# Graph block with experts on one core: edge lists kept in DRAM, deeper look-ahead in the middle stage, and the last node tile taken first

## The chip, the cores and the metric

The program runs on one core of a Trainium2 chip. The core has five engines with their own instruction lists: TensorE (PE, with its weight loads as PEld), VectorE (DVE), ScalarE (ACT), GpSimd (POOL) and SyncE (SP), which issues most of the transfers. The metric is the device time of one execution in microseconds (us), and the number compared is the median over runs. All times below are in us unless ns is written.

## The reference, cut to what matters

There are 6250 nodes with 256 features, 200000 edges sorted by destination, and 8 experts.

```python
xn = _layernorm(x)
x = x + gnn(edge_index, xn) + mix(xn)
x = x + ffn(_layernorm(x))

def gnn(A, X, W, b):                   # self-loops are added to A
    deg  = segment_sum(ones, dst)
    norm = rsqrt(deg)[src] * rsqrt(deg)[dst]
    return relu(segment_sum((X @ W)[src] * norm[:, None], dst) + b)

def mix(x):                            # linear attention, one sequence of all nodes
    q, k, v = split(x @ Wqkv.T);  q = elu(q) + 1;  k = elu(k) + 1
    t  = q @ sum(k v^T) / (q . sum(k) + 1e-6)       # per head, 8 heads of 32
    x1 = layer_norm(t + x)
    return layer_norm(gelu(x1 @ W1.T + b1) @ W2.T + b2 + x1)

def ffn(h):                            # one expert per token, capacity 977
    idx  = argmax(softmax(h @ gate_w + gate_b))
    pos  = running count of the tokens with that expert, in token order
    kept = pos < 977                   # the others get nothing
    return prob * expert[idx](h) * kept             # 256 -> 1024, relu -> 256
```

The running count ties the routing to the order of the tokens: which tokens fall beyond an expert's capacity depends on their place in the sequence, so tiles have to be routed in ascending order.

## The kernel before

The nodes lie in 49 tiles of 128 (tile 48 has 106 nodes). `twos` pairs them into 25 groups: group g holds tiles 2g and 2g+1, and the last group holds tile 48 alone. The program has three stages.

*Stage one* runs to about 295 us. It reads x, takes the layer norm's statistics, makes q, k and v (q goes to DRAM as `q_dram`), finds where each node's edges begin, and writes the normed, degree-scaled node rows to DRAM as `g_dram` (512 columns: the value in a high and a low part). It also makes the edge lists. For odd tiles these are `idx` (which row of `g_dram` to fetch) and `rel` (its place in the tile), and for even tiles `hiT` and `loT` (which source tile and which row in it, 110 columns for five tiles and each half). In the kernel before these four lists lie on chip for the whole of the main part. ScalarE copies each finished piece from PSUM into its list. Stage one ends with a flag, read from the device, and a branch (`tc.If`): when an edge list doesn't fit the fast form, a slow general path computes the sums instead and the lists are filled with values that match nothing. With these inputs the slow path isn't taken.

*Stage two* (about 300 to 1646 us) sums the neighbours' rows into every tile and finishes the nodes. Three generators share the engines, and the schedule is manual: within an engine, instructions run in the order in which the generators' steps are called.

- `gather()`, for the 24 odd tiles: 34 slots (EB) per tile, 816 in all. In slot j POOL issues an indirect DMA that fetches 128 rows into `gt` (L891) and VectorE makes a one-hot matrix `oh` from `rel` (L895). LAG slots later PE adds `oh` x `gt` into the PSUM tile `ps` (L906). A tile's sum starts with two matmuls of the tile's own rows (L903, L904). After slot 34, `put_sum` copies the left half out with ScalarE (L825) and adds the right half with VectorE (L827). The pool `ga` has GB buffers for `gt` and `oh`, the PSUM pool `gaps` has two for `ps`.
- `dense()`, for the 25 even tiles: a dense matrix of edge counts, tile by all 6250 source nodes, is built from one-hot pairs and then multiplied with all rows, which lie on chip in `xs3`. A unit (one tile) is 11 steps. In each step VectorE makes four pairs `lo`, `hi` (L838, L840), PE multiplies those of the step before into two PSUM banks `bp` (four matmuls, L874), ScalarE copies the banks into the matrix `A` (L875), and in the next unit PE does some 15 of the 147 matmuls `ps_d` (L858) of the matrix that is complete.
- `rounds()`: one round takes a group whose sums are there (c) through the GNN's matrix (L1067), layer norm and gate, the next group (b) through the second layer norm, and the one after it (a) through attention (L1099) and the MLP, each round being some 20 steps with `yield` between them. After every two groups `routing` turns the gate's values into slots of the experts' buffer and scatters the tokens to `xbuf` with one indirect DMA per tile (L984). Group 24, tile 48 alone, has a round and a routing of its own at the very end.

The loop that interleaves them calls one gather step per slot, and as many dense steps and round steps as keep the pace:

```python
        while any(alive.values()):
            step("g", G)
            while alive["d"] and done_d * (NGT + LAG) < n_dense * (j + 1):
                ...
            while alive["s"] and done_s < SIDE * (j + 1):
                ...
            j += 1
```

*Stage three* (from 1689 us) reads the experts' counts (L1207), loads each expert's tokens and weights, and computes two layers per expert (L1257, L1267), with a scatter to the output at the end (L1285).

Of the kernel before, what the change touches and what calls it, by code (L numbers as in the profile page):

```python
# [46 lines left out]
GB = 9  # L47
LAG = 7
SIDE = 0.74
# [13 lines left out]
def graph_block_kernel(  # L63
# [32 lines left out]
    deg_dram = dram.tile([AGR, 1], F32, name="deg_dram")  # L96
    q_dram = dram.tile([len(twos), P, 2, 2 * P], F32, name="q_dram")
# [3 lines left out]
    lists = main.enter_context(tc.tile_pool(name="lists", bufs=1))  # L101
    idx = lists.tile([P, NGC * P], I32, name="idx")
    rel = lists.tile([P, NGC * P], F32, name="rel")
    hiT = lists.tile([P, NDC, 2, 5 * NG], F32, name="hiT")
    loT = lists.tile([P, NDC, 2, 5 * NG], F32, name="loT")
# [356 lines left out]
    def edge_lists():  # L462
# [55 lines left out]
        for c in range(NGC):  # L518
            if c % 4 == 0:
                et = [rps.tile([P, 512], F32, name="et_ps", tag="et_ps", bufs=2) for _ in range(2)]  # L520
            gd, gs = got.pop(c)
            gf, gf2 = gd.bitcast(F32), gs.bitcast(F32)
            V.tensor_scalar(gf, gd, nfirst[:, c:c + 1], None, op0=OP.subtract)
            V.tensor_copy(gf2, gs)
            yield
            for e, w in zip(et, (gf, gf2)):
                nc.tensor.transpose(e[:, c % 4 * P:(c % 4 + 1) * P], w, ident)
            ask(c + 2)
            yield
            if c % 4 == 3 or c == NGC - 1:  # L530
                for o, e in zip((rel, idx), et):
                    nc.scalar.copy(o[:, (c - c % 4) * P:(c + 1) * P], e[:, :(c % 4 + 1) * P])
                yield
        for c in range(NDC):
# [18 lines left out]
            for v, o in ((kf, hiT), (lf, loT)):  # L553
                et_ps = rps.tile([P, 512], F32, name="et_ps", tag="et_ps", bufs=2)
                for h in range(2):
                    nc.tensor.transpose(et_ps[:, h * W:(h + 1) * W], v[:W, h * P:(h + 1) * P], ident[:W, :W])
                nc.scalar.copy(o[:, c].rearrange("p h g -> p (h g)"), et_ps[:, :2 * W])
# [150 lines left out]
    with tc.If(flag == 1):  # L708
        with tc.tile_pool(name="gp", bufs=1, side="right") as gp:
# [96 lines left out]
            V.memset(rel, -1.0)  # L806
            V.memset(hiT, 400.0)
# [3 lines left out]
    with tc.tile_pool(name="ga", bufs=GB, side="right") as ga, \  # L811
            tc.tile_pool(name="de", bufs=2, side="right") as de, \
            tc.tile_pool(name="gaps", bufs=2, space=PSUM) as gps, \
            tc.tile_pool(name="deps", bufs=1, space=PSUM) as dps, \
            tc.tile_pool(name="bups", bufs=2, space=PSUM) as bps, \
# [13 lines left out]

        def onehots(u, p):  # L830

            c, b = divmod(u, 5)
            o = []
            for g in (2 * p, 2 * p + 1):
                for h in range(2):
                    col = b * NG + g
                    lo = de.tile([P, P], BF16, name="lo", tag="lo", bufs=8)
                    V.tensor_scalar(lo, rowb, loT[:, c, h, col:col + 1], None, op0=OP.is_equal)  # L838
                    hi = de.tile([P, NB * GN], BF16, name="hi", tag="hi", bufs=8)
                    V.tensor_scalar(hi, hib, hiT[:, c, h, col:col + 1], None, op0=OP.is_equal)  # L840
                    o.append((lo, hi))
            return o

        def dense():

            mats, made = {}, None
            acc_ps = None
            half = NG // 2
            for u in range(ND + 1):
                for p in range(half):  # L850
                    if u >= 1 and p >= 1:

                        A = mats[u - 1]
                        if p == 1:
                            acc_ps = dps.tile([P, D], F32, name="ps_d", tag="ps_d")
                        for hi in range((p - 1) * NB // (half - 1), p * NB // (half - 1)):
                            for h in range(3):
                                nc.tensor.matmul(acc_ps, A[:, hi, :], xs3[:, hi, h * D:(h + 1) * D],  # L858
                                                 start=(hi == 0 and h == 0), stop=(hi == NB - 1 and h == 2))
                    coming = None  # L860
                    if u < ND:
                        if p == 0:
                            mats[u] = de.tile([P, NB, P], BF16, name="A", tag="A")
                        coming = (u, p, onehots(u, p))
                    if made is not None:
                        uu, pp, oh = made
                        for i in range(2):
                            g = 2 * pp + i
                            w = GN if g < NG - 2 else 4
                            at = GN * g if g < NG - 1 else P - 4  # L870
                            bp = bps.tile([P, 512], F32, name="bp", tag="bp")
                            for h in range(2):
                                lo, hi = oh[2 * i + h]
                                nc.tensor.matmul(bp[:, :NB * GN], lo, hi, start=(h == 0), stop=(h == 1))  # L874
                            nc.scalar.copy(mats[uu][:, :, at:at + w],  # L875
                                           bp[:, :NB * GN].rearrange("p (s k) -> p s k", k=GN)[:, :, :w])
                        if pp == half - 1:

                            V.tensor_tensor(mats[uu][:, 2 * uu, :], mats[uu][:, 2 * uu, :], identb, op=OP.add)
                    made = coming  # L880
                    if u >= 1 and p == half - 1:
                        put_sum(2 * (u - 1), acc_ps)
                    yield

        def gather():
            tiles = {}
            ps = None
            for j in range(NGT + LAG):
                if j < NGT:
                    gt = ga.tile([P, 2 * D], FR, name="gt", tag="gt")  # L890
                    nc.gpsimd.indirect_dma_start(  # L891
                        out=gt, out_offset=None, in_=g_dram,
                        in_offset=bass.IndirectOffsetOnAxis(ap=idx[:, j:j + 1], axis=0))
                    oh = ga.tile([P, P], FR, name="oh", tag="oh")
                    V.tensor_scalar(oh, rowb, rel[:, j:j + 1], None, op0=OP.is_equal)  # L895
                    tiles[j] = (gt, oh)
                i = j - LAG
                if i >= 0:
                    k, e = divmod(i, EB)
                    t = 2 * k + 1  # L900
                    if e == 0:
                        ps = gps.tile([P, 2 * D], F32, name="ps", tag="ps")
                        nc.tensor.matmul(ps, identb, xs3[:, t, :2 * D], start=True, stop=False)  # L903
                        nc.tensor.matmul(ps[:, D:], identb, xs3[:, t, 2 * D:], start=False, stop=False)  # L904
                    gt, oh = tiles.pop(i)
                    nc.tensor.matmul(ps, oh, gt, start=False, stop=(e == EB - 1))  # L906
                    if e == EB - 1:
                        put_sum(t, ps)
                yield
# [4 lines left out]
        def routing(batch, lgt, slots):  # L914

            tiles = [(gi, i) for gi in batch for i in range(twos[gi][1])]
            m = len(tiles)
            t0 = twos[batch[0]][0]
# [5 lines left out]
            def a3(name):  # L924
                return small([P, 4, N_EXP], name)[:, :m, :]

            def a2(name):
                return small([P, 4], name)[:, :m]
# [24 lines left out]
            fore = small([P, 5, N_EXP], "fore")  # L953
# [20 lines left out]
            for gi in batch:  # L974
# [5 lines left out]
            put = small([P, 4], "put", dtype=I32)  # L980
# [10 lines left out]
        def rounds():  # L991


            NGR = len(twos)
            xts, qs, ss, slots = {}, {}, {}, {}
            lgt = None

            def load(gi):
                if gi < NGR:
# [19 lines left out]
            for k in range(-2, NGR):  # L1019
                a = k + 2 if k + 2 < NGR else None  # L1020
                b = k + 1 if 0 <= k + 1 < NGR else None
                c = k if k >= 0 else None
# [3 lines left out]
                if a is not None:  # L1026
                    load(a + 1)
# [48 lines left out]
                if c is not None:  # L1076
                    slot = slots[c] = mx.tile([P, 2, ROW], F32, name="slot", tag="slot", bufs=3)
# [65 lines left out]
                if c is not None:  # L1143
# [5 lines left out]
                    if lgt is None:  # L1149
                        lgt, batch = small([P, 4, N_EXP], "lgt"), []  # L1150
                        if cr < P:
                            V.memset(lgt, 0.0)
                    at = 2 * len(batch)
                    batch.append(c)
# [5 lines left out]
                if c is not None:  # L1160
                    V.tensor_tensor(lgt[:cr, at:at + cn, :], lp[:cr, :cn * N_EXP].rearrange("p (t e) -> p t e", e=N_EXP),
# [12 lines left out]
                if c is not None and (len(batch) == 2 or c == NGR - 1):  # L1174
# [4 lines left out]
        n_dense = (ND + 1) * (NG // 2)  # L1179
# [11 lines left out]
        while any(alive.values()):  # L1191
            step("g", G)
            while alive["d"] and done_d * (NGT + LAG) < n_dense * (j + 1):
# [147 lines left out]
```

## Time and profile before

| | |
|---|---|
| runs, us | 2054.58, 2057.87, 2075.5; median 2057.87 |
| profiled execution, us | 2051.43, of which the span of the profile is 2049.6 |
| granted TensorE clock, mean | 0.905 |
| PE / PEld busy | 1648.4 us (80%) / 1203.4 us (59%) |
| DVE / ACT / POOL busy | 1275.3 us (62%) / 700.4 us (34%) / 924.3 us (45%) |
| moved by DMA | 337.83 MB, 165 GB/s over the span |
| costliest groups | gathers on POOL L891 794.8 us in 816; dense matmuls L858 489.4 us in 3675; one-hots `hi` L840 351.0 us in 1100; gather matmuls L906 335.1 us in 816 |

Busy shares are means over the whole span, and the three stages differ, so a share says little of what a single stage waits for. In the views of the profile a group is written as line, engine and operation, with `out<-in` by the program's names; "idle before, releaser" is the time in which the engine stood still ahead of such an instruction, with what ended it. "issue" there is time in which the engine waited for nothing that the profile shows. PEclk is the granted clock of TensorE in tenths of full speed.

### The profile page before, as it was taken

How to read it: one execution, taken by the hardware profiler on the slowest of the kernel's cores; microseconds unless marked ns; L12 is line 12 of the kernel's file. 1: busy time of each engine (PE TensorE's matmuls, PEld its weight loads, DVE VectorE, ACT ScalarE, POOL GpSimd, SP SyncE). 2: the span in 40 equal slices, each digit the busy share in tenths (PEclk: the TensorE clock that was granted, in tenths of full speed). 3: DMA queues.
4: the chain of work that ended last, by engine and by line, in shares of the span. 5: the costliest groups of instructions: out<-in, count | busy, mean ns of one | idle time of the engine just before them, and what ended most of it. 6: DMA issues, size and time to landing. Idle time of an engine off the chain costs nothing. (4 is left out here: it accounts for less than half of the span.)

```text
span 2049.6 us, 28653 instructions
## 1 busy us (share of the span) xinstructions
PE 1648.4 (80%) x9171; PEld 1203.4 (59%) x9171; DVE 1275.3 (62%) x5337; ACT 700.4 (34%) x1627; POOL 924.3 (45%) x957
## 2 busy tenths in 40 slices
PE   5787866887888888887878787887878737999996
PEld 2454544666666666665656565665656525586774
DVE  5767657677767778686757677776867431232332
ACT  2657952233333333232323232332323112233332
POOL 1022006666666666656656666665665610011111
PEclk9888997999998989898989899898999958999998
DMA  7346767777776677767767676667676615414220
GB/s 214 100 133 196 253 182 194 181 183 196 184 187 173 182 182 189 194 161 193 187 180 180 183 181 169 171 185 183 171 179 170 172 35 188 174 49 146 99 96 19
DMA packets 211319, 337.83 MB, mean 165 GB/s; under 512 B 30047, under 2 KB 79002, under 8 KB 211018
## 3 DMA queue, kind: packets, MB, share of 16 engines
q0 software_dynamic: 125424, 232.93, 44.3%
q1 hardware_dynamic: 85434, 101.74, 15.5%
q8 instruction: 81, 1.33, 0.3%
q10 hardware_dynamic: 288, 1.08, 0.1%
q14 instruction: 92, 0.75, 0.1%
HBM read 278.29 MB, written 60.06 MB: 165 GB/s over the span
## 5 line engine op out<-in xcount | busy, mean ns | idle before, releaser
L891 POOL DMA_INDIRECT gt<-g_dram,idx x816 | 794.8, 974 | 576.1 <-issue 168.7
L858 PE MATMUL ps_d<-xs,A 128*128 128x256 bf16 x3675 | 489.4, 287 | 41.3 <-issue 37.5
L875 ACT CAST A<-bp 128x294 bf16<-128x294 f32 (+1 forms) x550 | 200.6, 401 | 832.8 <-PE bp L874 231.0
L858 PEld LDWEIGHTS <-A 128*128 128x128 bf16 x3675 | 355.5, 103 | 171.5 <-issue 112.9
L906 PE MATMUL ps<-gt,oh 128*128 128x512 f32 x816 | 335.1, 484 | 42.6 <-DMA gt<-g_dram,idx 32.3
L840 DVE TENSOR_SCALAR hi<-hib,hiT 128x294 bf16<-128x294 bf16 x1100 | 351.0, 323 | 1.1 <-issue 1.1
L874 PE MATMUL bp<-hi,lo 128*128 128x294 bf16 x1100 | 216.0, 305 | 120.2 <-ACT A L875 39.6
L838 DVE TENSOR_SCALAR lo<-rowb,loT 128x128 bf16<-128x128 bf16 x1100 | 269.9, 245 | 3.2 <-PE ps_d L858 1.2
L895 DVE TENSOR_SCALAR oh<-rowb,rel 128x128 fp32r<-128x128 bf16 x816 | 207.2, 288 | 76.2 <-remote 30.4
L874 PEld LDWEIGHTS <-lo 128*128 128x128 bf16 x1100 | 109.6, 102 | 180.9 <-issue 57.3
L906 PEld LDWEIGHTS ps<-gt,oh 128*128 128x128 f32 x816 | 153.3, 206 | 76.5 <-DMA gt<-g_dram,idx 37.4
L1285 POOL DMA_INDIRECT out<-rep,who x43 | 42.4, 986 | 314.7 <-DVE rep L1283 226.8
L1257 PE MATMUL hpf<-xet,w1e 128*128 128x512 f32 (+2 forms) x544 | 154.1, 441 | 8.7 <-ACTq L1297 3.5
L1267 PE MATMUL ypf<-w2e,hm 128*128 128x256 f32 (+1 forms) x688 | 151.3, 379 | 0.0
L1267 PEld LDWEIGHTS ypf<-w2e,hm 128*128 128x128 f32 (+1 forms) x688 | 128.9, 188 | 21.9 <-issue 3.1
L1257 PEld LDWEIGHTS hpf<-xet,w1e 128*128 128x128 f32 x544 | 86.5, 193 | 70.0 <-issue 62.9
L1269 DVE TENSOR_TENSOR y<-ypf,fb_s 128x256 f32<-128x256 f32 (+1 forms) x43 | 18.2, 423 | 138.8 <-PE ypf L1267 138.8
L662 PE MATMUL mm<-wqkv_s,xnt 128*128 128x512 f32 (+1 forms) x196 | 101.5, 644 | 0.0
L1259 ACT ACTIVATE hm<-hpf,fb_s 128x512 f32<-128x512 f32 (+2 forms) x136 | 70.9, 525 | 84.6 <-PE hpf L1257 81.2
L1051 DVE TENSOR_SCALAR z<-mm 128x8 f32<-128x8 f32 (+1 forms) x49 | 7.9, 162 | 138.6 <-remote 82.6
L984 POOL DMA_INDIRECT xbuf<-slot,put x49 | 51.8, 1058 | 74.5 <-issue 45.4
L1101 ACT ACTIVATE s<-s,nb,rs 128x256 f32<-128x256 f32 (+1 forms) x98 | 53.6, 599 | 47.3 <-DVE rs_sr L194 29.8
(289 smaller groups left out, 2034.1 us busy)
## 6 DMA issues: line engine op xcount, KB each, us to landing
gt<-g_dram,idx POOLq DMA_INDIRECT x816
g_dram<-two SPq DMA_DIRECT2D x24, 512.0 KB
xt<-in_x SPq DMA_DIRECT2D x42, 256.0 KB
xbuf<-zeros SPq DMA_DIRECT2D x26, 384.0 KB
xe<-xbuf SPq DMA_DIRECT2D x8, 1028.0 KB
w1e<-in_fw SPq DMA_DIRECT2D x8, 1024.0 KB
w2e<-in_fw SPq DMA_DIRECT2D x8, 1024.0 KB
xe<-xbuf SPq DMA_DIRECT2D x8, 771.0 KB
```

The costliest lines, as they stand in the source:

```text
L662: nc.tensor.matmul(kp[:r, :], xnt[:, c, i * r:i * r + r], wqkv_s[:, c, D:3 * D], start=(c == 0), stop=(c == 1))
L838: V.tensor_scalar(lo, rowb, loT[:, c, h, col:col + 1], None, op0=OP.is_equal)
L840: V.tensor_scalar(hi, hib, hiT[:, c, h, col:col + 1], None, op0=OP.is_equal)
L858: nc.tensor.matmul(acc_ps, A[:, hi, :], xs3[:, hi, h * D:(h + 1) * D], start=(hi == 0 and h == 0), stop=(hi == NB - 1 and h == 2))
L874: nc.tensor.matmul(bp[:, :NB * GN], lo, hi, start=(h == 0), stop=(h == 1))
L875: nc.scalar.copy(mats[uu][:, :, at:at + w], bp[:, :NB * GN].rearrange("p (s k) -> p s k", k=GN)[:, :, :w])
L891: nc.gpsimd.indirect_dma_start(out=gt, out_offset=None, in_=g_dram, in_offset=bass.IndirectOffsetOnAxis(ap=idx[:, j:j + 1], axis=0))
L895: V.tensor_scalar(oh, rowb, rel[:, j:j + 1], None, op0=OP.is_equal)
L906: nc.tensor.matmul(ps, oh, gt, start=False, stop=(e == EB - 1))
L1257: nc.tensor.matmul(hp[:, :nn], w1e[:, c, f * P:(f + 1) * P], xet[:, c, at:at + nn], start=(c == 0), stop=(c == 1))
L1259: nc.scalar.activation(hm[:, f, :nn], hp[:, :nn], AF.Relu, bias=fb1_s[:, e * 8 + f:e * 8 + f + 1])
L1267: nc.tensor.matmul(yp[:r, :], hm[:, f, (i - i0) * P:(i - i0) * P + r], w2e[:, f, :], start=(f == 0), stop=(f == DFF // P - 1))
```

## The change

The four edge lists move from on-chip memory to DRAM tensors (`idx_l`, `rel_l`, `hi_l`, `lo_l`). Stage one writes each piece into a staging tile and stores it by DMA. Stage two loads the lists back in chunks, two buffers each, a chunk ahead of their use. On the slow path the fill values are stored in the same way.

In stage two the gathers run 9 slots ahead in 11 buffers (7 in 9 before). The one-hot pairs of a dense step are made two steps ahead of their matmuls, in 12 buffers each (one step, 8 buffers). The PSUM pool of `ps` has one bank instead of two, that of `bp` three instead of two, and `gather` has an extra `yield` ahead of each odd tile but the first. The share of round steps per slot, SIDE, is 0.72 instead of 0.74.

The dense units begin with tile 48 and go on with 0, 2, ... 46 (before 0, 2, ... 48). The rounds begin with group 24 (tile 48), whose gate values and token rows are kept in tiles of their own (`lgt_h`, `slot_h`); it is routed together with groups 22 and 23, the last two, as five tiles in ascending order.

```diff
-GB = 9
-LAG = 7
-SIDE = 0.74
+GB = 11
+LAG = 9
+SIDE = 0.72
...
+    idx_l = dram.tile([P, NGC * P], I32, name="idx_l")
+    rel_l = dram.tile([P, NGC * P], F32, name="rel_l")
+    hi_l = dram.tile([P, NDC, 10 * NG], F32, name="hi_l")
+    lo_l = dram.tile([P, NDC, 10 * NG], F32, name="lo_l")
...
-    lists = main.enter_context(tc.tile_pool(name="lists", bufs=1))
-    idx = lists.tile([P, NGC * P], I32, name="idx")
...
-                nc.scalar.copy(o[:, c].rearrange("p h g -> p (h g)"), et_ps[:, :2 * W])
+                st = rw.tile([P, 512], F32, name="st", tag="st")
+                nc.scalar.copy(st[:, :2 * W], et_ps[:, :2 * W])
+                nc.sync.dma_start(o[:, c, :], st[:, :2 * W])
...
-            tc.tile_pool(name="gaps", bufs=2, space=PSUM) as gps, \
+            tc.tile_pool(name="gaps", bufs=1, space=PSUM) as gps, \
             tc.tile_pool(name="deps", bufs=1, space=PSUM) as dps, \
-            tc.tile_pool(name="bups", bufs=2, space=PSUM) as bps, \
+            tc.tile_pool(name="bups", bufs=3, space=PSUM) as bps, \
...
+        def part(name, source, dtype=F32):
+            t = chunks.tile([P, source.shape[-1]], dtype, name=name, tag=name)
+            nc.sync.dma_start(t, source)
+            return t
...
+        gather_lists(0)
+        dense_lists(NDC - 1)
+        dense_lists(0)
+        gather_lists(1)
+
+        def node_tile(u):
+            return (2 * u - 2) % (2 * ND)
...
-                    lo = de.tile([P, P], BF16, name="lo", tag="lo", bufs=8)
+                    lo = de.tile([P, P], BF16, name="lo", tag="lo", bufs=12)
...
+            for n in range((ND + 1) * half + 2):
+                u, p = divmod(n, half)
+                if u < ND:
+                    ...
+                    made.append((u, p, onehots(u, p)))
+                m = n - 2
+                if m < 0:
+                    yield
+                    continue
+                u, p = divmod(m, half)
...
+                    c, w = divmod(j, P)
+                    if w == P // 2 and c:
+                        gather_lists(c + 1)
...
                     if e == 0:
+                        if k:
+                            yield
                         ps = gps.tile([P, 2 * D], F32, name="ps", tag="ps")
...
+            order = [NGR - 1] + list(range(NGR - 1))
...
+                    if c == NGR - 2:
+                        V.tensor_copy(lgt[:, 4, :], lgt_h)
+                        batch.append(NGR - 1)
...
-                if c is not None and (len(batch) == 2 or c == NGR - 1):
+                if c is not None and cn > 1 and len(batch) >= 2:
                     yield from routing(batch, lgt, slots)
...
-        n_dense = (ND + 1) * (NG // 2)
+        n_dense = (ND + 1) * (NG // 2) + 2
+        n_gather = NGT + LAG + NGB - 1
...
-            while alive["d"] and done_d * (NGT + LAG) < n_dense * (j + 1):
+            while alive["d"] and done_d * n_gather < n_dense * (j + 1):
```

## The prediction

> **What bounds the kernel now.** I read the page first: its top, then the slices.
>
> ```profile
> span 2049.6 us, 28653 instructions
> PE 1648.4 (80%) x9171; PEld 1203.4 (59%) x9171; DVE 1275.3 (62%) x5337; ACT 700.4 (34%) x1627; POOL 924.3 (45%) x957
> ...
> PE   5787866887888888887878787887878737999996
> DVE  5767657677767778686757677776867431232332
> POOL 1022006666666666656656666665665610011111
> PEclk9888997999998989898989899898999958999998
> ```
>
> A slice is 51 us. POOL's digits show three stages: up to about 300 us (statistics, lists), to 1646 us (gather, dense and rounds together), then the experts. The change touches the middle one and both its edges. The second view cuts that stage; its columns are length, busy us (instructions) of PE, PEld, DVE, ACT and POOL, granted clock, DMA share, GB/s.
>
> ```profile
> 300.00:340.00 40.00, 23.24 (x93) 14.48 (x94) 29.04 (x138) 11.70 (x27) 25.85 (x27) 0.71 0.74 191
> 440.00:1540.00 1100.00, 910.21 (x5780) 687.76 (x5779) 804.08 (x3671) 341.20 (x812) 688.19 (x703) 0.91 0.70 181
> 1600.00:1646.00 46.00, 34.82 (x211) 25.43 (x211) 15.70 (x59) 7.00 (x14) 27.57 (x29) 0.89 0.66 169
> 1646.00:1704.00 58.00, 14.74 (x48) 10.48 (x49) 17.75 (x93) 5.74 (x11) 5.61 (x5) 0.50 0.29 105
> ```
>
> In the body PE is busy 83%, DVE 73%, POOL 63%: TensorE leads, but stands idle a sixth of the time, and its clock of 0.91 means that 18% of the time runs at half rate. So I asked what PE waits for between 340 and 1646 us (reason: us in total, times, longest).
>
> ```profile
> PE bp L874 <- ACT A L875: 39.6, 26, 3.3
> PE ps_d L858 <- issue: 37.5, 49, 2.2
> PE ps L906 <- DMA gt<-g_dram,idx: 30.0, 22, 2.7
> PE bp L874 <- issue: 15.2, 24, 3.2
> PE bp L874 <- DVE hi L840: 13.7, 13, 2.1
> PE mm L1067 <- issue: 13.7, 4, 6.9
> ```
>
> Three kinds matter: histogram matmuls (bp) that wait for ScalarE to empty a bank, bp that wait for one-hots of VectorE, gather matmuls (ps) that wait for their rows. "issue" is none that a buffer cures. The last 46 us have only dense and gather work. Then comes the tail, in the timeline of POOL and DVE:
>
> ```profile
> 1672.49 0.98 POOL L984 DMA_INDIRECT xbuf<-slot,put  x1 [0.30 <-issue]
> 1682.13 1.60 POOL L984 DMA_INDIRECT xbuf<-slot,put  x1 [8.66 <-issue]
> 1689.28 0.16 DVE L1207 CAST counts<-base 1x8 int32<-1x8 f32 x1 [8.07 <-DMA xbuf<-slot,put]
> ```
>
> Four scatters of tiles 44 to 47 end with the first line; tile 48's comes 9.64 us later, and the experts' first instruction waits for its landing.
>
> **What the Trainium skill says.** "TensorE: Matmul & The Clock Gate", section on what is actually happening: the array runs at half clock after an idle window of about 3.4 us. The trace agrees: 0.50 in the idle tail, 0.91 in the body. The same page, Part 3 on packing small matmuls: matmuls start and end in program order. So a matmul that waits holds all behind it, gathers and dense alike; the 3.18 us in which PE stood before the bp at 1018.02 us, waiting for ScalarE, show it. "PSUM — Partial Sum Buffer", specifications: 8 banks per partition. The kernel before uses 3+2+1+2 and the changed one 3+1+1+3, so the third bp bank is the second ps bank; no trace line shows banks. "DMA: Bandwidth & Descriptors", anatomy of one DMA, gives a fixed cost of about 2 us per DMA, on GpSimd's path; no line shows a load the size of a list chunk, so I use 2.5 us as an estimate from that page.
>
> **The change, part by part.** The sums are against the profiled execution, 2051.43 us, which is 6.4 us under the median of the runs.
>
> *Tail.* Tile 48's round and routing leave the end. What was between the fourth scatter and the fifth (L1067 2.04 us, its norm, its routing) is gone; scatters follow each other every 1.3 us (1668.55, 1669.89, 1671.20, 1672.49), so the fifth starts at 1672.49+1.30, plus 0.2 for the fifth addition of fore: 1674.0 instead of 1682.13. Landing took 6.68 us, and what follows is unchanged: -8.1 us. What is late next is the landing of that same scatter. Certain within 1.5 us. The second half of its round (12 matmuls, about 2 us) moves into the body, where PE leads: +2.
>
> *One-hots two steps ahead, 12 buffers.* In the list of PE waits, bp waited for VectorE (hi 13.7, lo 8.5, and smaller ones at L1051, L1095, L191, L895, L956, L948, L950) 37.7 us, 1.1 us a time, longest 3.9. A dense step (4 bp, 15 ps_d, the gathers and rounds between) takes 1310/286 = 4.6 us; VectorE gains one whole step. It is 73% busy, so it can use it. I take -28 of 37.7 (bounds -10 and -38).
>
> *Third bp bank.* bp waits of 39.6 (A) and 4.8 (s, L1101) on ScalarE, 28 times. Each step fills two banks, so a third lets PE go on for one tile only: half of the 0.66 us that four bp take. 28 x 0.33 = -9 (bounds -5 and -25).
>
> *LAG 9, 11 buffers.* Gathers are issued two slots earlier: two slots are 2 x 1.59 us, more than the longest wait of 2.7. But 5.6 of the 30.0 us fall after 1596 us, where POOL issues every 1.25 us without a pause and no depth helps. I take -18 (bounds -5 and -24).
>
> These three are 55 us. PE goes on to the next wait in program order (75 to 80 us of "issue", and the ScalarE waits that stay), so I pass on 70%: -39 (bounds -14 and -61). PE idle in the stage is 17% of 1310, some 220 us; a fifth less idle should wake the clock more often. Half-rate time costs at most 0.09 x 1070 = 96 us; I take -6 (0 to -16).
>
> *One ps bank instead of two.* New wait: L903, the first matmul of the next odd tile, now waits for ScalarE's copy and VectorE's addition (L825, L827) of the last, 23 times, and all PE work is queued behind it. In the timeline of before the addition ended 0.9 to 7.2 us after the last gather matmul, mean 2.6 over 24. By the order of instructions the added yield puts a dense step (15 x 0.12 + 4 x 0.165 = 2.5 us) or more between in 16 of the 23 cases; in 7 there is 0 to 0.9 us. 7 x (2.2 less 0.35) = 13, and 16 cases of which three in ten overrun by 1.8 = 8: +21 (bounds +8 and +60).
>
> *Slower start.* Dense matmuls begin two dense steps later, at slot 41 instead of 34. Slots at that end are paced by POOL at 1.25 us: 6.7 x 1.25 = 8.4 us, in which PE does only some of what it has to do later. +5 (0 to 8).
>
> *Lists through memory.* Stage one: 14 stores on SP, 2 MB by the shapes. ScalarE leads there (46 us busy of 50 from 200 to 250 us) and SP waits for VectorE, so nothing waits for them unless a copy waits for its staging buffer: +1 (0 to 5). Stage edge: eight list loads precede x and q on SP, and no load is issued ahead of the branch any more. PE's first instruction now is an attend that waits for q, the tenth DMA: 299.23 + 9 x 0.42 + 2.5 = 305.5 us instead of 301.45; PE was mostly idle from 315 to 325 anyway: +2 (0 to 6). The later loads, 18 DMAs, sit half a chunk ahead of their use, with buffers long free: 0, covered by 64 slots, or 3 us each without that cover.
>
> The rest (order of routing, five tiles, SIDE 0.72 of 848 slots against 0.74 of 823, both about 610 round steps) is 0.
>
> Sum: -8.1 +2 -39 -6 +21 +5 +1 +2 = -22. From 2051.4 that is 2029; from the median of 2057.9 it is **2036 us**, 1.1% faster.
>
> **The rivals.** *Lookahead pays in full* (0.15): all 61 us, clock 16, ps bank at 8: -8-61-16+8+5 = -72, 1986. For it: VectorE and POOL have slack. Against: the "issue" waits and ScalarE's late copies stay.
> *Gains cancel* (0.12): a cured stall shows up as the next one, 30% passed on (-17), no clock: -8+2-17+21+8 = +6; about 2060. For it: PE's waits are spread over nine causes.
> *The single ps bank is the loss* (0.23): PE is tied to VectorE's and ScalarE's present place 23 times, and the one-hots now queued ahead of L827 on VectorE (8 more, 1.5 us) lengthen the chain from 2.6 us. At S us per switch the sum is -43 + 23 S, so it is even at 1.9 and 1% slower at 2.8. With S = 3 plus cold clock after each stall: +26 to +35, about 2088. For it: chains of 4.9 to 7.2 us occur in three of 24 cases. Against: 16 of 23 have cover.
> *The change doesn't move the last round*: the order of instructions excludes it; PE's list ends with one round and one routing.
>
> **How the numbers follow.** The forecast's own case has 0.50 and spans 2010 to 2058. About 1% (20 us) can be told from no change. Faster by over 1%: 0.27 of the forecast's case and 0.15 = 0.42; within 1%: 0.22 and 0.12 = 0.34; slower: 0.01 and 0.23 = 0.24. The range 1988 to 2085 leaves out half of the slow rival and half of the full payment, some 0.19, and holds both ends of the ps bank's cost.
>
> **What would show it.** Right: a single group of five scatters 1.3 us apart and some 8 us less from the last gather to the experts; bp waits on VectorE under 12 us; ps waits on DMA under 15; PE waits at the ps start (L952 after) of 10 to 30 us; PE's clock 0.91 or more. Wrong: waits at that matmul above 60 us, a gap of tens of us at 300 us, or bp waits on ScalarE and "issue" that grow by what the others lost.

## The result, and the profile after

| | before | after |
|---|---|---|
| median of 14 runs each, us | 2058.12 (2051.61 to 2075.5) | 2081.78 (2074.56 to 2089.03) |
| ratio, with 95% interval | | 1.0122 [1.0104, 1.0140] |
| profiled execution, us (span) | 2051.43 (2049.6) | 2088.62 (2086.8) |
| granted TensorE clock | 0.905 | 0.893 |

The changed kernel is 24 us slower. Its profiled execution lies 7 us above its own median and that of before 7 us below, so the two traces differ by 37 us. In some series of runs every kernel, that of before too, took some 180 us less, nearly all of it in stage two (before 1874 to 1877 us instead of 2053 to 2069), so each experiment below is given as a ratio to runs of before from its own series, and the two conditions are kept apart.

The page of the changed kernel, top and slices (52 us each):

```profile
span 2086.8 us, 28724 instructions
PE 1649.8 (79%) x9167; PEld 1207.1 (58%) x9167; DVE 1273.6 (61%) x5318; ACT 695.7 (33%) x1624; POOL 928.1 (44%) x957
...
PE   5786856687879787878787879787878846899996
...
PEclk9889987898989898989898989888889877999999
```

The busy times are those of before to within 1%. What grew is the time around them. The windows of the changed kernel, the last two cut at its own stage end (length; busy us and instructions of PE, PEld, DVE, ACT, POOL; clock; DMA share; GB/s):

```profile
300.00:340.00 40.00, 14.24 (x57) 9.54 (x58) 22.93 (x111) 8.12 (x19) 21.41 (x23) 0.69 0.74 197
440.00:1540.00 1100.00, 897.90 (x5707) 682.25 (x5705) 792.82 (x3616) 335.09 (x803) 670.18 (x680) 0.89 0.68 178
1647.00:1693.00 46.00, 33.92 (x196) 23.94 (x194) 11.63 (x44) 3.81 (x8) 27.80 (x29) 0.85 0.62 160
1693.00:1742.00 49.00, 7.54 (x31) 5.75 (x31) 10.35 (x53) 2.68 (x6) 5.63 (x5) 0.58 0.35 122
```

The first row lost 9 us of PE work at the stage's start. In the body POOL issues fewer instructions in the same 1100 us (680 against 703), so the stage runs 3% slower, and its clock is 0.89 instead of 0.91. The last row is the tail, shorter than before. In the timeline of POOL and DVE the tail looks like this:

```profile
1714.69 1.03 POOL L1033 DMA_INDIRECT xbuf<-slot,put  x1 [28.19 <-issue]
...
1718.63 0.99 POOL L1033 DMA_INDIRECT xbuf<-slot,put  x1 [0.30 <-issue]
1719.93 1.61 POOL L1033 DMA_INDIRECT xbuf<-slot_h,put  x1 [0.30 <-issue]
1727.27 0.16 DVE L1265 CAST counts<-base 1x8 int32<-1x8 f32 x1 [13.37 <-DMA xbuf<-slot_h,put]
```

Five scatters stand 1.3 us apart, and tile 48's (`slot_h`) is the last of them. The gather ends at 1692.8 us (before 1645.1) and PE's first transpose of the experts comes at 1741.4 (before 1703.05), so the tail fell from 58.0 to 48.7 us. The experts take the same time. All of the loss lies ahead of the gather's end, which is 47.7 us later.

PE's waits in stage two of the changed kernel (340 to 1692 us; total, times, longest):

```profile
PE ps_d L907 <- issue: 50.6, 61, 1.8
PE mm L208 <- ACT ag L836: 44.6, 11, 6.7
PE bp L918 <- ACT A L919: 38.4, 24, 5.9
PE ps L955 <- DMA gt<-g_dram,idx: 31.7, 28, 2.4
PE ps L952 <- DVE ag L838: 27.0, 8, 6.0
PE bp L918 <- DVE z L1105: 4.0, 1, 4.0
```

Of the histograms' waits for one-hots (hi 13.7, lo 8.5 before) none is left among the larger rows; all their waits for VectorE together are 8.6 us instead of 37.7. Two new waits stand there: the single bank's (L952, 27.0) and one that the prediction does not have at all, a round's first transposes, which wait for ScalarE's copy of a finished sum (L208, 44.6; before 9.9 in 4). Summed over the trace, the gaps between PE's matmuls from 340 us to the end of the gather are 230.5 us before and 261.4 after.

One of these new waits, in the timelines of PE and ScalarE:

```profile
730.30 1.58 PE L907 MATMUL ps_d<-xs,A 128*128 128x256 bf16 x13
731.72 0.66 PE L918 MATMUL bp<-hi,lo 128*128 128x294 bf16 x4
736.66 1.12 PE L208 MATMUL mm<-ident,ag 128*128 128x128 f32 x4 [4.04 <-ACT ag L836]
...
735.79 0.55 ACT L919 CAST A<-bp 128x196 bf16<-128x196 f32 x2 [5.46 <-remote]
736.22 0.39 ACT L836 COPY ag<-ps_d 128x256 f32<-128x256 f32 x1
```

The dense sum ends at 731.9 us and the histograms after it at 732.4, but ScalarE, idle for 5.46 us, begins its copies only at 735.8. PE stands behind them. The trace names nobody who released ScalarE ("remote"), but what it copies is PE's work, done for over 3 us. So it is not ScalarE that is busy too long; the news of PE's completion comes late. All 11 waits of this row are alike: ScalarE had been idle for 4.0 to 6.9 us before the copies.

### The profile page after: what moved, and what is told of

It is laid out like the page before. It is cut to its first block, busy times and chain, and to the rows that moved or that the text cites. A ratio compares the mean times of both kernels' runs of the same rounds, so it can differ in the third digit from the quotient of the medians.

```text
span 2086.8 us, 28724 instructions
## 1 busy us (share of the span) xinstructions
PE 1649.8 (79%) x9167; PEld 1207.1 (58%) x9167; DVE 1273.6 (61%) x5318; ACT 695.7 (33%) x1624; POOL 928.1 (44%) x957
## 4 chain that ended last, share of the span: by engine, by line
PE 37%; issue 18%; DVE 9%; DMA 8%; another core or an unknown queue 7%; ACT 3%; POOL 3%; SPq 0%; POOLq 0%; DVEq 0%; ACTq 0%
PE ps_d L907 14%; PE ps L955 7%; PE bp L918 6%; DMA out<-rep,who 5%; PE mm L1189 2%; PE mm L1224 2%; DVE hi L880 2%; PE mm L208 2%; DMA gt<-g_dram,idx 2%; ACT A L919 1%; DVE lo L878 1%; DVE oh L942 1%; PE mm L1121 1%; POOL gt L938 1%
## 5 line engine op out<-in xcount | busy, mean ns | idle before, releaser
L907 PE MATMUL ps_d<-xs,A 128*128 128x256 bf16 x3675 | 496.6, 289 | 50.7 <-issue 50.6
L955 PE MATMUL ps<-gt,oh 128*128 128x512 f32 x816 | 341.0, 491 | 38.0 <-DMA gt<-g_dram,idx 31.7
L918 PE MATMUL bp<-hi,lo 128*128 128x294 bf16 x1100 | 208.1, 308 | 61.3 <-ACT A L919 38.4
L1328 ACT ACTIVATE y<-y,xe 128x256 f32<-128x256 f32 (+1 forms) x43 | 21.9, 508 | 119.1 <-DVE y L1327 119.1
```

## The experiments

**e5 and e11, the changed kernel again, under both conditions.** No edit.

> The changed kernel itself, unchanged, beside the kernel before. In e1 to e4 the kernel before ran 180 us shorter than in the first comparison, and PE's completions reached the other engines without the bunches (83 in the middle stage of the first trace of before). Theory 3 (the loss hangs on those late completions: the transposes' 4 us stalls behind the dense tile, and the bank's, are the time until a late completion): without bunches the changed kernel is faster than before, ratio 0.985 to 0.995; with bunches it is 1.012 again. Rival (the loss is in the kernel's order, whatever the completions): ratio 1.01 either way.

> The changed kernel itself. Where PE's completions come in bunches: ratio 1.012 to 1.013 to before, as measured twice. Where they don't (before at 1875 us): theory 3 says faster than before, ratio 0.990 to 0.995, since e4 (0.990) and e9 (0.995) are near it; the rival, that the order costs the same there, says 1.005 or more.

Measured: e5 1.0131 [1.0108, 1.0154], with before at 2052.7 us; e11 0.991 [0.9885, 0.9934], with before at 1876.6 us. The same pair of kernels changes places with the condition. The same place in e11 (round after the same group), and below it the largest waits of PE in stage two there:

```profile
651.83 1.58 PE L907 MATMUL ps_d<-xs,A 128*128 128x256 bf16 x13
653.25 0.66 PE L918 MATMUL bp<-hi,lo 128*128 128x294 bf16 x4
654.60 0.66 PE L208 MATMUL mm<-ident,ag 128*128 128x128 f32 x4 [0.45 <-ACT ag L836]
...
653.70 0.57 ACT L919 CAST A<-bp 128x196 bf16<-128x196 f32 x2 [2.14 <-PE bp L918]
```

```profile
PE ps L955 <- DMA gt<-g_dram,idx: 67.5, 65, 3.0
PE ps L952 <- DVE ag L838: 19.5, 9, 5.8
...
PE mm L208 <- ACT ag L836: 4.8, 13, 0.5
```

ScalarE begins 0.04 us after the first pair of histogram matmuls, and the wait is 0.45 us instead of 4.04. Over all 550 bank copies, the time from the end of a pair of histogram matmuls to ScalarE's copy has a mean of 1.61 us in the trace of before and 2.00 in that of after (over 3 us: 120 and 128 copies); in e1 it is 0.08 (none over 3) and in e11 0.19 (6). Some of these copies stood behind other work of ScalarE, but before 58 of the 120 and 59 of the 128 it had just been idle for over 1 us, and before none of those in e11. PE's semaphore updates (its signals that a piece of work is done), too, come 97 times in groups of four or more, each within 60 ns of the one before, in stage two of the trace of before (the expectation above has 83); in e1 no two come closer than 70 ns. In the other direction nothing is late: where PE waited for VectorE or ScalarE, it starts a median of 0.05 us after their instruction's end, in the trace of before as in e1. So in the first condition PE's completions reach the other engines late and in bunches, in the second promptly. I call them *late* and *prompt* below.

Two reservations. The ends of matmuls in these traces are modelled, so a single delay is not exact. And the late traces lack part of the updates: before has 1725 of VectorE's 3434 in stage two and 439 of ScalarE's 882, e1 all but one. So the causes that a late trace names are uncertain. PE's waits for "issue" in stage two are 81.0 us before and 90.8 after, and in e1, e11 and e14 there is not one; in the late traces they may well be waits for updates that aren't recorded. What makes completions late, and whether their recording has a part in it, no run shows.

**e6, two banks for the gather's sums.** Late.

```diff
-            tc.tile_pool(name="gaps", bufs=1, space=PSUM) as gps, \
+            tc.tile_pool(name="gaps", bufs=2, space=PSUM) as gps, \
...
-            tc.tile_pool(name="bups", bufs=3, space=PSUM) as bps, \
+            tc.tile_pool(name="bups", bufs=2, space=PSUM) as bps, \
```

> The changed kernel with two banks for the gather's sums and two for the histograms (before: 2 and 2; changed: 1 and 3), the extra yield kept. The prediction's working: the single bank costs 21 us and the third histogram bank gains 9, so 12 us faster than the changed kernel. Rival (the extra yields cover the single bank, and the third bank of the histograms is what counts): 5 us or more slower than the changed kernel.

Measured: 1.0069 [1.0043, 1.0095], against 1.0131 of e5 in the same series: 13 us faster. The wait at L952 is gone (27.0 us in the changed kernel's trace, 25.2 in e5's); that of the histograms for ScalarE is 39.4 us with two banks, and with three it was 38.4 and 23.9. So the single bank costs more than the third one gives, and with late completions the exchange is about half of the loss.

**e3, e8, e12 and e15, the order of before.** The changed kernel with dense units 0 to 48, rounds 0 to 24 and the last routing alone.

```diff
-            return (2 * u - 2) % (2 * ND)
+            return 2 * u
...
-            order = [NGR - 1] + list(range(NGR - 1))
```

> The changed kernel with the order of before (dense 0 to 48, rounds 0 to 24, last routing alone), all else as changed. Theory 2: the tail costs 9 us again, the waits of the transposes for ScalarE's copy fall from 45 to under 15 us, so 15 to 30 us faster than the changed kernel, 2052 to 2067. Rival (the single ps bank and the lists are the whole loss): 8 us slower than the changed kernel, about 2090.

> e3 again (the changed kernel with the order of before). Theory 2 with bunches: the tail costs 9 us more, the transposes' stalls 28 us less, ratio 1.003. Rival (the order is not the loss): ratio 1.017, the tail's 9 us on top. Without bunches: 0.984 again.

> e3 and e8 again, beside the changed kernel on the same chip. With bunches, theory 2: 9 us of tail lost, 28 us of the transposes' stalls saved, ratio 1.003 (rival: 1.017). Without bunches: 0.984 to 0.988 again, and the difference to e11 says what the order costs there: theory 3 expects the order to gain its 9 us of tail (e11 faster), the numbers of e3 and e4 that it loses (e11 slower).

> The changed kernel with the order of before, wanted where PE's completions come in bunches. Theory 2: the tail costs 9 us, the transposes' stalls fall by 28, ratio 1.003 against 1.012 to 1.013 of the changed kernel. Rival (the order isn't the loss): 1.017. Without bunches: 0.984 to 0.988 again.

Measured, prompt: 0.9839 [0.981, 0.9868], 0.9878 [0.985, 0.9905], 0.9861 [0.9835, 0.9887]; e12 is 5 us (by the medians) to 9 us (by the ratios) faster than e11 in its series. Late (e15): 1.015 [1.0125, 1.0176]. So theory 2, that the order is the loss because it makes the dense tile the last to arrive, falls: with the old order the kernel is not faster but 4 us slower than e5 by the ratios, with intervals that overlap. PE's waits of e15 show what became of the stalls:

```profile
PE ps_d L905 <- issue: 60.7, 77, 2.5
PE bp L916 <- ACT A L917: 34.6, 22, 7.7
PE ps L950 <- DVE ag L838: 29.7, 13, 7.7
PE bp L916 <- issue: 23.3, 18, 6.8
PE mm L208 <- ACT ag L836: 21.1, 6, 4.9
PE ps L953 <- DMA gt<-g_dram,idx: 16.3, 13, 2.6
```

The wait of the transposes fell by nearly what was foretold (28), from 44.6 to 21.1 us, and its long stalls end with group 10, from which the odd tile is the last. But others grew by as much, and the gaps of PE in the stage add up to 266.3 us instead of 261.4. The old order also brings back the tail's 9 us, so a total of 4 us leaves up to 5 us of gain in the stage; the traces show none (the gather ends at 1692.4 us, against 1692.8 in the changed kernel's trace and 1686.4 in e5's). The 4 us stalls were real, and taking half of them away was worth 5 us at most, not 24.

**e4, e7 and e13, dense led by up to one unit.** All three prompt.

```diff
-            while alive["d"] and done_d * n_gather < n_dense * (j + 1):
+            while alive["d"] and done_d < n_dense * (j + 1) / n_gather + min(11.0, (j + 1) / 12):
```

> The changed kernel with the dense generator led by up to 11 steps, one unit, gained over the first 132 slots: the even tile is then ready before the odd one from about group 9, as before. Theory 2: the waits of the transposes for ScalarE's copy fall to some 15 us in the first ten rounds, so 20 to 30 us faster than the changed kernel, 2052 to 2062. Rival (PE is merely idle elsewhere, the stall is only where the slack shows): within 5 us of the changed kernel.

> e4 again (the changed kernel, dense led by up to one unit), wanted where PE's completions come in bunches. Theory 2: with the even tile ready ahead of the odd one from about group 9, the transposes' waits for ScalarE's copy fall from 45 to some 17 us, all before group 10: ratio to before 1.000, against 1.012 to 1.013 of the changed kernel. Rival (bunches stop PE elsewhere instead): the waits move to the histograms and the dense matmuls, ratio 1.008 or more. Without bunches: 0.990 again.

> e4 and e7 again (dense led by up to one unit), wanted where PE's completions come in bunches. Theory 2: even tiles ready first from about group 9, the transposes' waits for ScalarE's copy fall from 45 to some 17 us, all before group 10: ratio 1.000 against 1.012 to 1.013. Rival (bunches stop PE elsewhere instead): ratio 1.008 or more. Without bunches: 0.990 again.

Measured: 0.9902 [0.9875, 0.993], 0.9903 [0.9876, 0.993], 0.9903 [0.9867, 0.9938]: no difference from e11. No series of theirs was late, so these runs do not test what they were made for.

**e9, two more yields ahead of the transposes,** SIDE 0.78. Prompt.

```diff
+                if c is not None:
+                    yield
+                    yield
                 if a is not None:
                     load(k + 3)
```

> The changed kernel with two more yields between the moment at which a group's sums are called for and its transposes, so that some 4 us of other PE work stand between the dense tile's last matmul and them; SIDE 0.78 to make room for the 50 added steps. Theory 2: it doesn't matter which tile is last, only that PE has work until ScalarE's copy is there; the transposes' waits for that copy fall under 15 us and the ratio to 1.000 to 1.004 with bunches. Rival (the stall comes from PE's own bunched completions, which any full queue meets): waits of the same size one step later, ratio over 1.010.

Measured: 0.9952 [0.9931, 0.9974]: slower than e7 (0.9903) in the same series. Where the copy comes promptly there is nothing to cover, and the added steps, with the SIDE that makes room for them, cost 8 us against e7 by the medians.

**e10, the dense lead and two banks.** Prompt.

> e7 with two banks for the gather's sums and two for the histograms. If the two causes add: 13 us (e6) and some 25 us (e7) off the changed kernel, ratio 0.994 with bunches. If the waits share their time (PE finds the next stall in either): no more than 5 us better than e7.

Measured: 0.9899 [0.9872, 0.9926], the same as e7: with the dense lead the exchange of banks is worth nothing where completions are prompt. (Without the lead, e14 below, with two and two banks, has 0.9814, and the three prompt runs of e3, e8 and e12, with one and three, have 0.984 to 0.988; that would be some 8 us, but the runs are from different series.)

**e1, e2 and e16, the kernel before with lists in DRAM, and with lists and order.** All prompt. e1 has only the DRAM tensors, stores, chunks and loads of the diff; e2 and e16 add `node_tile`, `order`, `lgt_h`, `slot_h` and the joint routing. Look-ahead, banks and paces are those of before.

> The kernel before with its four lists in DRAM and loaded in chunks, nothing else changed. Theory 1 (the loads after the branch hold up the start of stage two: first gather 5.7 us later and PE's first matmul 14 us later in the changed kernel): some 8 us slower than before, about 2066, with the whole of it lost by slot 60 and none after. The prediction's sum: 3 us slower, 2061. A rival in which list loads in the body delay gathers: slower by more than 15 us, growing over the stage.

> e1 plus the order alone: tile 48 first in the dense units and the rounds, its routing joined with the last two groups'; look-ahead, banks and paces as before. Theory 2 (with one more unit ahead of tile 0, every dense tile is ready after its odd neighbour, so each round's first transposes stand at PE right behind the dense tile's last matmuls and wait there for ScalarE's copy): the tail gives 9 us back, the transposes' waits grow by 25 to 45 us, so 15 to 35 us slower than e1, about 2090. The prediction's sum (tail -8, half a round +2): 6 us faster than e1, about 2060.

> e2 again: lists in DRAM and the new order, but look-ahead, banks (two and two) and paces of before. It differs from e6 (ratio 1.007 with bunches) by the look-ahead alone: gathers 9 instead of 7 ahead, one-hots two steps instead of one ahead in 12 instead of 8 buffers. Theory 4, after e15 overthrew theory 2 (with bunches PE stands waiting for its own late completions, so deeper look-ahead buys nothing): ratio 1.003 to 1.010, within 8 us of e6. The prediction's sum (look-ahead -39 us less the third bank's share, some -32): ratio 1.022. Without bunches: 1.001 again, where look-ahead is worth 2% (e1 and e2 against e14).

Measured: e1 1.0026 [1.0009, 1.0042]; e2 1.0006 [0.9983, 1.0029]; e16 1.0022 [1.0006, 1.0038]. The lists cost some 5 us, between the 3 of the prediction and the 8 of theory 1. The order then gains 1 to 4 us, with intervals that overlap, not the 6 of the prediction (and with the look-ahead, e11 against e12, it costs a little). No late series has these kernels.

**e14, old order and two and two banks.** Prompt.

> The changed kernel with the order of before and with two and two banks; against e6 it differs by the order alone. With bunches, theory 2: the tail costs 9 us, the transposes' stalls fall by 28, so ratio 0.998 against 1.007 of e6; rival (the order isn't the loss): 1.011. Without bunches: as e12, 0.986, within 0.003.

Measured: 0.9814 [0.9781, 0.9847], the fastest there. It differs from e1 by the look-ahead (gathers 9 ahead, one-hots two steps ahead, with the yields and paces that belong to it) alone, though in another series: 2.1%, or 40 us, by the ratios. PE's largest waits in stage two, of e1 and then of e14:

```profile
PE ps L948 <- DMA gt<-g_dram,idx: 83.8, 83, 3.0
PE bp L912 <- DVE hi L878: 14.0, 14, 3.7
PE mm L1002 <- DVE fore L998: 9.8, 9, 2.2
PE bp L912 <- DVE lo L876: 5.3, 11, 1.8
```

```profile
PE ps L953 <- DMA gt<-g_dram,idx: 66.6, 62, 3.2
PE mm L208 <- ACT s L1148: 21.4, 28, 5.4
PE mm L1007 <- DVE fore L1003: 9.0, 8, 2.9
```

With prompt completions the histograms' waits are gone and those for rows are 17 us less, while the transposes wait 21.4 us for ScalarE instead of 0.3. In kind this is what the prediction expected of the look-ahead. The size, 40 us against its 39 and 6, agrees in part by chance: the two traces lie 29 us apart, and PE's gaps in stage two differ by only 17.5 us (122.1 and 104.6), its busy time by 12.9.

**e17 and e18, e14 with one half of the look-ahead taken back.** Both late.

```diff
-GB = 11
-LAG = 9
+GB = 9
+LAG = 7
```

```diff
-                    lo = de.tile([P, P], BF16, name="lo", tag="lo", bufs=12)
+                    lo = de.tile([P, P], BF16, name="lo", tag="lo", bufs=8)
...
-                m = n - 2
+                m = n - 1
```

> e14 (old order, two and two banks: 0.981 without bunches) with gathers 7 ahead in 9 buffers instead of 9 in 11. The prediction: 18 us of waits for rows, 70% of it passed on, so 13 us slower than e14. Without bunches: 0.988, if the waits for rows (64 us in e12's profile) come back in part; with bunches, theory 4 says 1.009, the same as e6 less the order's 5 us gain, and the prediction 1.016.

> e14 with the one-hots one step ahead in 8 buffers instead of two in 12. The prediction: 28 us of waits for VectorE, 70% of it passed on, so 20 us slower than e14. Without bunches: 0.991; with bunches, theory 4 says 1.009, the prediction 1.019.

Measured: e17 1.0002 [0.9984, 1.0019]; e18 1.0034 [1.0019, 1.0049]. e14 itself was in no late series. Its ratio there can only be estimated by adding: e15 less what the banks gave (1.0150 - 0.0062), 1.009, good to some 0.005. Against that, taking either half of the look-ahead back did not cost 13 or 20 us; both kernels are faster than the estimate, e17 by 18 us and e18 by 11. For e18 that is about the error of the estimate. So the deeper gathers and the earlier one-hots, worth 40 us together with prompt completions, show no gain with late ones, and together they may cost; that rests on the estimate. Theory 4, that the look-ahead buys nothing where PE waits for its own late completions, expected nothing either way.

## Why the prediction went wrong, by its own steps

- **Tail, -8.1.** Right: -9.3 in the two traces, from the scatters that it named.
- **Lists +1 and +2, slower start +5.** Nearly right in sum. e1 shows 5 us for the lists instead of 3, with prompt completions. But PE's first matmul after the branch, foretold for 305.5 us instead of 301.5, comes at 316.1 in this trace and at 310.8 in e11, where the wait is put down to the load of q. That load, the tenth, is issued at 309.5 (304.2) and not at 303.0, and PE starts 6.5 us after it in both, where the prediction put 2.5. From the first gather to slot 59's matmul it is 97.5 us before and 100.3 after, so the slower start is some 3 us; the 6.7 us between there and slot 60 are the first of the transposes' stalls.
- **Single bank +21, third bank -9.** The net, 12, is right with late completions: e6 measured 13. The wait at the switch was 27.0 us for 23 switches, S = 1.2 us. The rival named after the bank wanted 3 us a switch; that its 2088 lies near the measured time is not its doing.
- **One-hots -28, gathers -18.** The waits for VectorE went as foretold, from 37.7 to 8.6 us. The waits for rows did not: 30.0 us before, 31.7 after, where under 15 was foretold.
- **70% of 55 passed on, -39, and -6 for the clock.** This is the step that failed. The three shortened waits were credited with 39 us less time and a better clock, as though each wait were a cause of its own, and the 75 to 80 us of "issue" a kind apart. Measured, nothing of the 39 arrived. PE's gaps rose from 230.5 to 261.4 us although the histograms' part of them fell from 101.4 to 60.3; the transposes' rose from 18.9 to 64.4, the single bank's from 0 to 30.4, the dense matmuls' from 41.3 to 50.7. e15 shows the same exchange in the other direction. The clock fell to 0.89 with the gaps, instead of rising. The account that fits is that many of these waits have one cause, PE's completions that reach the other engines some microseconds late: a matmul that no longer waits for a one-hot then waits for the next thing that a late completion holds back, a bank, a sum's copy, the transposes. What is shown is that the look-ahead gains 40 us where completions are prompt, and that no gain shows where they are late. That late completions are what takes the gain away is argued from the traces; no run set the lateness by itself.

With nothing for the failed step (and for the third bank, which it contains), the prediction's own sum is -8 +2 +21 +5 +1 +2 = +23; measured is +24. That is closer than it deserves, and in part luck, since e6 puts the exchange of banks at 13 instead of 21, and e1 and e2 the order at less than its -6. What is left over may be the look-ahead's own cost, to which e17 and e18 point, but that rests on an estimate. The rival "gains cancel" came nearest to what happened, but still passed on 30%. With prompt completions the changed kernel gains 0.9%, 17 us of 1876, where the prediction said 22.

The evidence was in the trace of before. The 3.18 us in which PE stood before the bp at 1018.02 us are given in the prediction as time spent "waiting for ScalarE":

```profile
1013.42 0.72 PE L874 MATMUL bp<-hi,lo 128*128 128x294 bf16 x4
1014.11 0.23 ACT L936 ACTIVATE pr<-pr 128x32 f32<-128x32 f32 x1 [1.06 <-DVE red L932]
1017.56 0.71 ACT L875 CAST A<-bp 128x294 bf16<-128x294 f32 x2 [3.22 <-remote]
1018.02 0.97 PE L874 MATMUL bp<-hi,lo 128*128 128x294 bf16 x4 [3.18 <-ACT A L875]
```

The matmuls of these banks end at 1014.14 us. ScalarE is done with a small instruction at 1014.34 and stands idle for 3.22 us before it copies. So PE waited for ScalarE, and ScalarE for the news of PE's own work. What was missing was the question when the copy could have begun.

## What to carry to other kernels

Before a wait for another engine is credited as removable, look at that engine in the timeline: if it too is idle and starts microseconds after the producer's end, the wait is for the producer's completion, and curing one consumer can hand the time to the next. Then count the total idle time of the bounding engine, not its list of waits; e15 halved a stall of 45 us and gained 5 us at most. Moving a bank from an accumulator that is switched 23 times to the histograms cost 13 us here with late completions.

## What the runs showed of the hardware

- From the end of a pair of histogram matmuls to ScalarE's copy it takes 0.04 us (median) and 0.08 (mean) in e1, and 0.77 (median) and 1.61 (mean) in the trace of before, ScalarE's other work included. The changed kernel against before is then 0.9% faster or 1.3% slower (e11, e5). One and the same chip showed both conditions in different series (e7 to e10 prompt, e17 and e18 late), so it isn't a property of a chip; what sets it is open.
- With prompt completions TensorE is granted 0.92 to 0.94 of its clock over the whole span instead of 0.89 to 0.91. For the changed kernel itself, with no edit, it is 0.937 (e11) and 0.896 (e5), and PE's gaps in stage two are 114.3 and 261.7 us: gaps and clock go together. Which of them leads the other no run shows. From 340 us to the end of the gather the traces of before and e1 are 176 us apart: PE's gaps make 108 of them, and 68 are longer busy time for the same work, at a clock of 0.91 and 0.96.
